# Fold products by column halves, an earlier fetch of source rows and one more batch of picks in a graph attention kernel

## The chip, the cores and the metric

The kernel runs on one core of a Trainium2 chip. The metric is the device time of one execution in microseconds (us); three runs give 1699.82, 1701.03 and 1702.28, median 1701.03. All numbers on single instructions come from one profiled execution.

## The reference

One layer of a graph network: 6250 nodes with 64 values each, 206250 edges sorted by destination, four heads of 16 values. The inputs `x`, `src`, `dst`, the edges' own values and the weights are given.

```
Qh, Kh, Vh = x @ W.T + b            # for each node, [N, 4, 16]
Ee = edge_attr @ We.T + be          # for each edge
score = (Kh[src] * Qh[dst] / 4 * Ee).sum(-1)
score = exp(clip(score, -5, 5))
wV = segment_sum(Vh[src] * score, dst)
out = layernorm(x + wV)
```

So for each edge the key and value row of its source is fetched, multiplied with the query of its destination, and the result is summed over the edges of one destination.

## The kernel before

**Tiles, groups, steps.** 128 edges are a tile, 8 tiles a group: 1612 tiles, 202 groups, the last of 4 tiles. Groups go in steps: two groups each at first, one each for the last eight (`STEPS`). A table of key and value rows of all nodes (`kv_tab`) is made first, then the main loop over `g` (line 983) runs an order written out by hand; each engine works off its own instructions in that order. Semaphores join them.

**Rows of the sources** come in two ways. POOL fetches a tile's 128 rows by an indirect DMA (`gather_kv`, L276), five steps of buffers ahead at most (`KVB`), one instruction per tile. Two tiles of most groups are not gathered but *picked*, that is, computed on TensorE: one batch makes four tiles, two each of two groups (`PICKED`). For a batch the source numbers are loaded to all partitions (`fetch_sources`, L236, a 256 KB DMA on SP's queue with two buffers), turned into `from`, `over` (ACT, L241, L242) and `odd` (DVE, L243) by `sources`; then DVE compares them with the node numbers (`hots`, L681) and PE multiplies these one-hot columns with the nodes' values `x`, held as three bf16 parts (`picks`, through `product`, L725, output `pick`). A batch has 25 units; a unit is three products of 128 rows by 512 columns (two for the last). 35 units go into 4 groups. After the last unit of a batch follow `picked` (DVE, L703), `picked_kv` (eight f32 products, `pick<-w,x`) and `place_kv` (ACT, L720), which writes the picked rows to the same buffers as the gathers do.

`LAST` (line 91) is the number of batches: as long as the group that ends a batch's units is more than 8 groups from the end. Here there are 67; the last units stand in group 192, and the last picked groups are 196 and 197. `BEGIN` and `READY` are the groups with a batch's first and last unit. 1304 gathers are left, besides the five first groups, whose rows are fetched otherwise.

**One iteration `g`** (lines 983 to 1092), as far as it matters here. SP: edges (`et`, every second group), sources if the next group begins a batch (line 994), queries (`qw`), keys (`kb`). PE: up to four units of picks, the turn of group `g+1` (L761: transposes `term` to `qe`), queries of `g+2` (`qq`), the other picks, a fold if one is due, the sums of a step (`sums`, `room<-msg,of`, 64-column halves in turn), edge products of `g+3` (`room<-et,we_sb`, four quadrants). DVE: `prod` and `score` of group `g` (`products`, L787, L789), what is left of the message of `g-1` (`take`, L827), the term of `g+1` (`terms`, L755), one-hot columns, the message of `g` (L808), and the adds. ACT: scores, copies (`keep`, L822), biases and one-hot rows. The gathers for the step four ahead are tied to marks on PE's products (`gather`).

**Folds.** Sums of a step land in a ring of 64-row blocks. After every some eight groups (24 times in all; `FOLDS`) `fold_blocks` brings two blocks of 128 rows together on PE, in f32: for each half `u` of the columns one product with `fold` (64 columns wide, L725 `room<-ring,fold`) and, into the first 31 rows of the same half, one or two with `ident` (`room<-ring,ident`). An f32 product is two instructions. Both halves stand in one PSUM bank, in partitions 0 to 63 and 64 to 127; `add_blocks` (L927) adds them to the output.

**The end.** From iteration 193 on there are no picks. Iterations 200 and 201 finish the last two groups; `last_add` (L963), the norms and two stores of the output (L959) follow.

Of the kernel before, what the change touches and what calls it, by code (L numbers as in the profile page):

```python
# [24 lines left out]
NG = -(-T // G)  # L25
# [32 lines left out]
def tiles_of(g):  # L58
    return min(G, T - g * G)
# [13 lines left out]
UNITS = NB // 2  # L73
# [7 lines left out]
def first_unit(g):  # L81

    return (g - LEAD) * 35 // 4


def when(k):

    return max(g for g in range(LEAD + 4 * k // 35 + 2) if first_unit(g) <= k)


LAST = max(m for m in range(1, NG) if when(UNITS * m - 1) + 8 < NG)
BEGIN = [when(UNITS * m) for m in range(LAST)]
READY = [when(UNITS * m + UNITS - 1) for m in range(LAST)]
PICKED = [(READY[m] + 4, READY[m] + 5) for m in range(LAST)]
ALL_PICKED = {g for pair in PICKED for g in pair}
assert len(ALL_PICKED) == 2 * LAST and min(ALL_PICKED) > XG
assert all(BEGIN[m + 1] > BEGIN[m] + 1 for m in range(LAST - 1))

# [36 lines left out]
def tile_gnn(ctx: ExitStack, tc: tile.TileContext, x, x_blocks, by_rows, xT, wT, bias, beT, weT, eT, src, src_rows, dst,  # L135
# [19 lines left out]
    def kv_of(g):  # L155

        s = max(s for s in range(NS) if STEPS[s][0] <= g)
        j = (g - STEPS[s][0]) * G
        return kvs[s % KVB][:, j:j + G, :]
# [52 lines left out]
    def fetch_edges(q):  # L212

        lo, hi = q * LG * G // 2, min((q + 1) * LG * G, T) // 2
        et = loads.tile([P, LG * G // 2, P], F32, name="et")
        nc.sync.dma_start(et[:, :hi - lo, :], eT[:, lo:hi, :])
        for g in range(q * LG, min((q + 1) * LG, NG)):
            ET[g] = et[:, (g % LG) * G // 2:(g % LG + 1) * G // 2, :]
# [13 lines left out]
    def fetch_sources(m, pool):  # L232

        if m < LAST:
            SRC[m] = pool.tile([P, BATCH * P], I32, name="srcs")
            nc.sync.dma_start(SRC[m], src_rows[m:m + 1, :].to_broadcast([P, BATCH * P]))  # L236
# [67 lines left out]
    with tc.tile_pool(name="nodes", bufs=1) as nodes, \  # L304
# [13 lines left out]
        slots = [kv.rearrange("p t c -> p (t c)") for kv in kvs]  # L318
# [163 lines left out]
        for i in range(NB // CB):  # L482
            bs = slice(i * CB, (i + 1) * CB)
            kv_sb = chunks.tile([P, CB, 2 * C], F32, name="kv_sb")
            for b in range(0, CB, 2):
                two = slice(i * CB + b, i * CB + b + 2)
                ps = npsum.tile([P, 2, 3 * C], F32, name="ps")
                for u in range(2):
                    c0 = (i * CB + b + u) * P
                    mark.append(nc.tensor.matmul(ps[:, u, :], xT_sb[:, c0:c0 + P], w_sb, start=True,  # L490
                                                 stop=True))
# [135 lines left out]
    with tc.If(rv == 0) as branch:  # L627

        with tc.tile_pool(name="work", bufs=2) as work, \
# [87 lines left out]
            def place_kv(m):  # L717
                for i, g in enumerate(PICKED[m]):
                    n = tiles_of(g)
                    nc.scalar.activation(kv_of(g)[:, n - 2:n, :], rooms_of(m)[:, 2 * i:2 * i + 2], AF.Copy)  # L720
# [3 lines left out]
            def product(*aps, **kw):  # L724
                mark.append(nc.tensor.matmul(*aps, **kw))  # L725
# [25 lines left out]
            def terms(g):  # L751

                n = tiles_of(g) // 2
                TERM[g] = work.tile([P, G // 2, P], F32, name="term")
                nc.vector.tensor_mul(TERM[g][:, :n], EB.pop(g)[:, :n], qq[:, :n])  # L755
# [24 lines left out]
            def some_of(g):  # L780

                n = tiles_of(g)
                return [(0, n)] if g < NG - 1 else [(0, n // 2), (n // 2, n)]

            def products(g, lo, hi):
                prod = work.tile([P, G, C], F32, name="prod", bufs=1)[:, :hi - lo, :]
                nc.vector.tensor_mul(prod, kv_of(g)[:, lo:hi, :C], qe[g % 2][:, lo:hi, :])  # L787
                SCORE[g] = work.tile([P, G, H], F32, name="score", bufs=3)[:, :hi - lo]
                nc.vector.tensor_reduce(SCORE[g], prod.rearrange("p g (h d) -> p g h d", h=H),  # L789
                                        axis=AX.X, op=OP.add)  # L790

            def weigh(g, lo, hi):
                score = SCORE.pop(g)
                nc.scalar.activation(score, score, AF.Relu, bias=five_p, scale=-1.0)  # L794
                WEIGHT[g] = weights[g % 3][:, lo:hi]
                nc.scalar.activation(WEIGHT[g], score, AF.Exp, bias=five_p, scale=-1.0)  # L796
# [23 lines left out]
            def keep(g, i):  # L820
                left, part = part_of(g, i)
                nc.scalar.activation(part, left, AF.Copy)  # L822
# [79 lines left out]
            def slots(lo, apart):  # L902

                ks = [k for k in (lo, lo + 2) if k in touched]
                if not apart and len(ks) == 2 and ks[0] % RING < ks[1] % RING:
                    return [(0, 2, ring[:, ks[0] % RING:ks[1] % RING + 1:2, :])]
                return [((k - lo) // 2, (k - lo) // 2 + 1, ring[:, k % RING:k % RING + 1, :]) for k in ks]

            def fold_blocks(i):

                for u in range(2):
                    whole = slots(4 * i + u, False)
                    for lo, hi, what in whole:
                        product(folded[u * C:(u + 1) * C, lo:hi], fold, what, start=True, stop=False,
                                skip_group_check=True)
                    for lo, hi, what in slots(4 * i + u - 1, i == len(ENDS) - 1):
                        product(folded[u * C:u * C + SHIFT, lo:hi], ident[:, C:C + SHIFT], what,
                                start=hi > max(h for _, h, _ in whole), stop=True, skip_group_check=True)

            def add_blocks(i):  # L920

# [61 lines left out]
            for g in range(NG + 1):  # L983
                now, before = g < NG, g > 0
# [6 lines left out]
                    going = alone(going[:2] if g == groups_of(step_of[g])[0] else going[2:])  # L991
                if g % LG == 0 and g + 3 * LG < NG:
                    fetch_edges(g // LG + 3)
                if g + 1 in BEGIN[1:]:
                    fetch_sources(BEGIN.index(g + 1) + 1, work)
                if g + 4 < NG:
                    fetch_queries(g + 4)
                if g % 2 == 0 and g + 6 < NG:
# [5 lines left out]
                where.append(mark[-1])  # L1004
                if former:
                    keep(g - 1, 1)
                if now:
                    products(g, *some_of(g)[0])
                if former:
                    take(g - 1, 1)  # L1010
                if g + 1 < NG:
                    terms(g + 1)
                if now:
                    weigh(g, *some_of(g)[0])
                if g + 2 < NG:
# [36 lines left out]
                if g in FOLDS:  # L1052
                    fold_blocks(FOLDS[g])
# [219 lines left out]
```

## Time and profile before

| | |
|---|---|
| median of three runs | 1701.03 us |
| the profiled execution | 1701.22 us |
| its span, first to last instruction | 1699.4 us |
| granted clock of TensorE, mean | 0.982 |
| gathers on POOL | 1304 of 946 ns |
| picks on PE | 4958 products |
| folds | 24 |

A busy share is that of the whole span. In a row of the page stand line, engine, operation, what it writes and reads, the count, the busy time with the mean of one, and the idle time just before with what ended most of it. In a row of the timeline stand the start, the length, engine, line and operation; a number in brackets is the engine's idle time just before, and what ended it. Rows of the stretches hold the stretch, its length, busy time of PE, weight loads, DVE, ACT and POOL, the granted clock, and the DMA engines' share and GB/s.

### The profile page before, as it was taken

What the parts mean: (1) busy time and instruction counts of PE and PEld (TensorE: products, weight loads), DVE (VectorE), ACT (ScalarE), POOL (GpSimd) and SP (SyncE); (2) the same over time, 40 slices, a digit from 0 to 9 for tenths busy, and PEclk for the clock granted to TensorE, in tenths of its full rate; (3) what the DMA queues carried; (4) which work ended last, traced back from release to release, by engine and by line L of the source; (5) the groups of instructions that cost most, each with busy time, mean ns of one, the idle gap of its engine ahead of it and who ended that gap; (6) DMA issues with size and microseconds to landing.
All of it is one profiled execution on the core that took longest, in us unless ns stands there. A gap on an engine that the chain in (4) does not pass through costs nothing.

```text
span 1699.4 us, 29987 instructions
## 1 busy us (share of the span) xinstructions
PE 1641.8 (97%) x10327; PEld 818.4 (48%) x10327; DVE 1525.8 (90%) x2588; ACT 1097.8 (65%) x1860; POOL 1272.5 (75%) x1354
## 2 busy tenths in 40 slices
PE   7799999999999999999999999999999999999975
PEld 6444444444444444444444444444444444444443
DVE  5699989899989899998998998989999999889986
ACT  3676666666666666666666666666666666666664
POOL 7777777777777777777777777777777777777775
PEclk9799999999999999999999999999999999999995
DMA  6744344343443434434434344443444433434341
GB/s 195 244 123 143 99 123 123 104 124 109 114 123 104 123 108 114 124 117 123 114 108 130 99 122 122 106 124 105 117 123 117 123 111 111 123 105 130 111 116 46
DMA packets 115090, 203.90 MB, mean 120 GB/s; under 512 B 55216, under 2 KB 55961, under 8 KB 114815
## 3 DMA queue, kind: packets, MB, share of 16 engines
q1 hardware_dynamic: 71484, 113.99, 22.1%
q0 software_dynamic: 43008, 86.86, 19.3%
q8 instruction: 83, 1.36, 0.3%
q10 hardware_dynamic: 436, 1.04, 0.3%
q14 instruction: 79, 0.65, 0.1%
HBM read 194.18 MB, written 7.59 MB: 119 GB/s over the span
## 4 chain that ended last, share of the span: by engine, by line
PE 80%; DVE 7%; DMA 7%; issue 2%; ACT 2%; POOL 1%; SPq 0%; DVEq 0%; ACTq 0%; POOLq 0%
PE pick L725 59%; PE room L725 11%; PE qe L761 5%; DMA kv<-kv_tab,src_i 4%; PE qq L725 3%; DMA srcs<-in_src_rows 2%; POOL kv L276 1%; DVE prod L787 1%; DVE msg L827 1%; DVE term L755 1%; PE ps L490 1%; DVE hot L681 1%; DVE score L789 1%; DVE qe L827 1%; DVE of L775 1%
## 5 line engine op out<-in xcount | busy, mean ns | idle before, releaser
L276 POOL DMA_INDIRECT kv<-kv_tab,src_i x1304 | 1233.1, 946 | 398.1 <-issue 173.8
L725 PE MATMUL pick<-hot,parts 128*128 128x512 bf16 x4958 | 1136.4, 380 | 0.0
L725 PEld LDWEIGHTS <-parts 128*128 128x128 bf16 x4958 | 459.5, 98 | 588.1 <-issue 90.3
L681 DVE TENSOR_TENSOR hot<-from,still 128x2560 bf16<-128x2560 bf16 (+4 forms) x415 | 481.7, 1164 | 2.4 <-ACT still L796 2.4
L822 ACT ACTIVATE msg<-qe 128x512 bf16<-128x512 f32 x400 | 237.8, 594 | 170.2 <-DVE qe L808 98.8
L740 ACT ACTIVATE eb<-room,be_col 128x512 f32<-128x512 f32 x202 | 136.8, 677 | 147.1 <-PE room L725 146.6
L262 ACT ACTIVATE to<-to,one_p 126x1024 bf16<-126x1024 bf16 x198 | 226.9, 1146 | 0.0
L256 ACT ACTIVATE to<-kb,minus_row 126x1024 bf16<-126x1024 uint8 x198 | 224.7, 1135 | 0.0
L794 ACT ACTIVATE score<-score,five_p 128x32 f32<-128x32 f32 x203 | 65.1, 321 | 147.8 <-DVE score L789 145.9
L761 PE MATMUL qe<-ident,term 128*128 128x128 f32 x806 | 125.7, 279 | 28.1 <-DVE term L755 26.4
L787 DVE TENSOR_TENSOR prod<-kv,qe 128x512 f32<-128x512 f32 x203 | 137.1, 676 | 12.0 <-PE qe L761 3.7
L789 DVE TENSOR_REDUCE score<-prod 128x32 f32<-128x512 f32 x203 | 138.5, 682 | 7.0
L827 DVE TENSOR_TENSOR qe<-qe,msg 128x512 f32<-128x512 f32 x200 | 138.2, 691 | 3.9 <-ACT msg L822 3.8
L808 DVE SCALAR_TENSOR_TENSOR qe<-still,kv 128x512 f32<-128x512 f32 x200 | 138.7, 693 | 0.8 <-ACT still L796 0.8
L827 DVE TENSOR_TENSOR msg<-qe,msg 128x512 bf16<-128x512 f32 x200 | 136.6, 683 | 3.1 <-ACT msg L822 2.6
L755 DVE TENSOR_TENSOR term<-eb,qq 128x512 f32<-128x512 f32 x202 | 136.6, 676 | 3.0 <-DMA kv<-kv_tab,src_i 2.6
L725 PE MATMUL room<-et,we_sb 64*64 64x256 f32 (+1 forms) x1616 | 136.2, 408 | 0.3 <-ACT eb L740 0.2
L761 PEld LDWEIGHTS qe<-ident,term 128*128 128x128 f32 x806 | 99.9, 143 | 75.8 <-DVE term L755 41.9
L243 DVE TENSOR_SCALAR odd<-srcs 128x512 int32<-128x512 int32 x66 | 30.2, 458 | 79.4 <-DMA srcs<-in_src_rows 79.3
L725 PE MATMUL room<-msg,of 128*64 128x192 bf16 (+1 forms) x1592 | 88.6, 251 | 1.6 <-DVE y L927 1.3
L725 PEld LDWEIGHTS <-of 128*64 128x64 bf16 (+1 forms) x1600 | 67.4, 110 | 39.0 <-issue 36.6
L241 ACT ACTIVATE from<-srcs,from_row 128x512 bf16<-128x512 int32 x66 | 47.3, 717 | 60.0 <-DMA srcs<-in_src_rows 60.0
(156 smaller groups left out, 1102.9 us busy)
## 6 DMA issues: line engine op xcount, KB each, us to landing
et<-in_eT SPq DMA_DIRECT2D x100, 512.0 KB
kb<-key_tab SPq DMA_DIRECT2D x101, 252.0 KB
kv<-kv_tab,src_i POOLq DMA_INDIRECT x1304
srcs<-in_src_rows SPq DMA_DIRECT2D x67, 256.0 KB
qw<-q_tab SPq DMA_DIRECT2D x202, 15.8 KB
kv_tab<-kv_sb SPq DMA_DIRECT2D x4, 640.0 KB
q_tab<-q SPq DMA_DIRECT2D x5, 480.0 KB
out<-y SPq DMA_DIRECT2D x2, 512.0 KB
```

The costliest lines, as they stand in the source:

```text
L256: nc.scalar.activation(TO[g][:, :n, :], KB.pop(g)[:, :n * P].rearrange("p (j e) -> p j e", j=n), AF.Square, bias=minus_row3[:3 * W])
L262: nc.scalar.activation(TO[g][:, :n, :], TO[g][:, :n, :], AF.Relu, bias=one_p[:3 * W], scale=-1.0)
L276: return nc.gpsimd.indirect_dma_start(out=kv_of(g)[:, j, :], out_offset=None, in_=kv_tab[:, :], in_offset=bass.IndirectOffsetOnAxis(ap=src ...
L681: nc.vector.tensor_tensor(HOT[k][:, lo_ - lo:hi_ - lo].rearrange("p b (a c) -> p b a c", c=2), pairs(from_)[:, None].to_broadcast(shape), ...
L725: mark.append(nc.tensor.matmul(*aps, **kw))
L755: nc.vector.tensor_mul(TERM[g][:, :n], EB.pop(g)[:, :n], qq[:, :n])
L761: nc.tensor.transpose(qe[g % 2][:, k:k + half + 1:half, :], TERM[g][:, k, :], ident)
L787: nc.vector.tensor_mul(prod, kv_of(g)[:, lo:hi, :C], qe[g % 2][:, lo:hi, :])
L789: nc.vector.tensor_reduce(SCORE[g], prod.rearrange("p g (h d) -> p g h d", h=H), axis=AX.X, op=OP.add)
L808: nc.vector.scalar_tensor_tensor(to.rearrange("p g (h d) -> p g h d", h=H), WEIGHT.pop(g)[:, :, :, None].to_broadcast([P, n, H, D]), LEAST ...
L822: nc.scalar.activation(part, left, AF.Copy)
L827: nc.vector.tensor_sub(left if i == 0 else part_of(g, 2)[1], left, part)
```

## The change

There are four edits.

1. `LAST` goes by 5 instead of 8 groups from the end. That makes 68 batches. The units of the new one stand in groups 192 to 195. `PICKED` lies four groups behind `READY` as before, but no further than group 199: the new batch fills two tiles each of groups 199 and 200. The other batches stay as they are.
2. `fold_blocks` makes the `fold` products of both halves first and then the `ident` products of both; before, one half came after the other.
3. `fetch_sources` is called two groups ahead of `BEGIN`, not one.
4. In iteration 200 alone (`NG - 2`) `products` comes behind `take` and `terms`.

```diff
-LAST = max(m for m in range(1, NG) if when(UNITS * m - 1) + 8 < NG)
+LAST = max(m for m in range(1, NG) if when(UNITS * m - 1) + 5 < NG)
-PICKED = [(READY[m] + 4, READY[m] + 5) for m in range(LAST)]
+PICKED = [(r + k, r + k + 1) for r in READY for k in [min(4, NG - 2 - r - 1)]]
...
             def fold_blocks(i):
 
+                whole = [slots(4 * i + u, False) for u in range(2)]
                 for u in range(2):
-                    whole = slots(4 * i + u, False)
-                    for lo, hi, what in whole:
+                    for lo, hi, what in whole[u]:
                         product(folded[u * C:(u + 1) * C, lo:hi], fold, what, start=True, stop=False,
                                 skip_group_check=True)
+                for u in range(2):
                     for lo, hi, what in slots(4 * i + u - 1, i == len(ENDS) - 1):
                         product(folded[u * C:u * C + SHIFT, lo:hi], ident[:, C:C + SHIFT], what,
-                                start=hi > max(h for _, h, _ in whole), stop=True, skip_group_check=True)
+                                start=hi > max(h for _, h, _ in whole[u]), stop=True,
+                                skip_group_check=True)
...
-                if g + 1 in BEGIN[1:]:
-                    fetch_sources(BEGIN.index(g + 1) + 1, work)
+                if g + 2 in BEGIN[1:]:
+                    fetch_sources(BEGIN.index(g + 2) + 1, work)
...
-                if now:
+                if now and g != NG - 2:
                     products(g, *some_of(g)[0])
                 if former:
                     take(g - 1, 1)
                 if g + 1 < NG:
                     terms(g + 1)
+                if g == NG - 2:
+                    products(g, *some_of(g)[0])
                 if now:
                     weigh(g, *some_of(g)[0])
```

## Prediction

> **What bounds the kernel now.** I read the page first, then who waited for whom, the busy time by stretches, and the timeline around one fold and at the end.
>
> ```profile
> span 1699.4 us, 29987 instructions
> PE 1641.8 (97%) x10327; PEld 818.4 (48%) x10327; DVE 1525.8 (90%) x2588; ACT 1097.8 (65%) x1860; POOL 1272.5 (75%) x1354
> L276 POOL DMA_INDIRECT kv<-kv_tab,src_i x1304 | 1233.1, 946 | 398.1 <-issue 173.8
> ```
> ```profile
> POOL kv L276 <- issue: 173.8, 568, 0.5
> ```
>
> POOL looks 75% busy, but the gather row says otherwise: 1304 gathers, 946 ns each, and 398.1 us idle before them, which is 0.305 us for each one. The longest such gap was 0.5 us. So POOL issues a gather every 1.25 us from its first to its last and never really waits: it is full, and its last gather can only come earlier if there are fewer.
>
> ```profile
> 115.00:1636.00 1521.00, 1514.05 (x9679) 733.26 (x9678) 1396.56 (x2274) 995.29 (x1646) 1150.14 (x1217) 1.00 0.41 117
> 1636.00:1683.00 47.00, 26.13 (x205) 15.68 (x203) 40.11 (x85) 31.84 (x54) 35.42 (x39) 0.79 0.32 89
> PE qe L761 <- DVE term L755: 5.7, 11, 1.0
> ```
>
> From 115 to 1636 us PE is busy 1514 of 1521 us (the first column behind the stretch's length), and waits for DVE 5.7 us in all (the waits of that same stretch). So the long middle goes at PE's pace. Then the picks end, PE falls to 26 of 47 us, and DVE (40 of 47) sets the pace. How far POOL leads can be read from the last gather of a group and the group's `prod` (L787, one per group in order; gathers counted back from the last, 4, 8 or 6 to a group): here group 189 and group 200.
>
> ```profile
> 1585.23 0.94 POOL L276 DMA_INDIRECT kv<-kv_tab,src_i  x1 [0.30 <-PE pick L725]
> 1605.55 0.69 DVE L787 TENSOR_TENSOR prod<-kv,qe 128x512 f32<-128x512 f32 x1
> ...
> 1680.09 0.94 POOL L276 DMA_INDIRECT kv<-kv_tab,src_i  x1 [0.30 <-issue]
> 1683.09 0.69 DVE L787 TENSOR_TENSOR prod<-kv,qe 128x512 f32<-128x512 f32 x1 [3.13 <-issue]
> ```
>
> The lead is 20.3 us at group 189 and gone at group 200: there DVE idles 3.13 us and starts 3.0 us after the last gather began. I read that 3.0 as the landing. So **two clocks meet at group 200**: POOL's gathers, and the chain of PE and DVE, which would have been ready at 1683.09 - 3.13 = 1679.95. From there 16.3 us follow to the end at 1699.4.
>
> **The change, part by part.**
>
> *Fewer gathers.* With the sixth last group as bound there are 68 batches, not 67. The new one picks two tiles each of groups 199 and 200, so POOL does 1300 gathers. Four times 1.25 is 5.0 us. Two go before group 199's last gather and two before group 200's, so group 200's data can be there at 1683.09 - 5.0 = 1678.1, and group 201's also 5.0 earlier. Nothing on POOL hides or adds to this.
>
> *More picks.* The new batch has 25 units, 24 of three products and one of two: 74 products, in iterations 192 to 195, where none or few stand now.
>
> ```profile
> 1628.81 0.60 PE L761 MATMUL qe<-ident,term 128*128 128x128 f32 x4
> 1629.68 3.41 PE L725 MATMUL pick<-hot,parts 128*128 128x512 bf16 x15
> 1633.02 0.66 PE L725 MATMUL room<-et,we_sb 64*64 64x256 f32 x8
> ...
> 1639.30 0.66 PE L761 MATMUL qe<-ident,term 128*128 128x128 f32 x4 [1.10 <-DVE term L755]
> 1642.43 1.16 PE L725 MATMUL pick<-w,x 128*128 128x128 f32 x8 [1.40 <-ACT pick L714]
> 1645.25 0.66 PE L761 MATMUL qe<-ident,term 128*128 128x128 f32 x4 [1.66 <-DVE term L755]
> 1650.25 0.66 PE L761 MATMUL qe<-ident,term 128*128 128x128 f32 x4 [1.38 <-DVE term L755]
> 1655.90 0.68 DVE L755 TENSOR_TENSOR term<-eb,qq 128x512 f32<-128x512 f32 x1
> ```
>
> A run of 15 picks takes 1633.02 - 1629.68 = 3.34 us, 0.223 each; 74 are 16.5 us. All stand between the turns (L761) of group 192 (1628.81) and group 196 (1650.25). In that stretch PE waits 1.10 + 1.40 + 1.66 + 1.38 = 5.5 us, which the picks fill; so group 196's turn comes 16.5 - 5.5 = 11 us later. DVE, which now trails PE there, has caught up by then: behind that turn (0.66) it has prod, score, take and term, some 2.5 us, and ends group 197's term at 1650.25 + 11 + 0.66 + 2.5 = 1664.4, against 1655.90 + 0.68 = 1656.6 now: 7.8 later. The new batch's `x` (L703, 0.74 for one in the tail) comes after that. I take 8.5 us; the bounds are 11.7 (nothing caught up) and 2 (the hots, 7.7 us a batch by the row below, less the waits of 5.5 us). That POOL itself slows under more DVE work can be left out: its gathers take 0.94 us beside the hots and in the tail alike.
>
> ```profile
> L681 DVE TENSOR_TENSOR hot<-from,still 128x2560 bf16<-128x2560 bf16 (+4 forms) x415 | 481.7, 1164 | 2.4 <-ACT still L796 2.4
> 842.93 0.43 PE L725 MATMUL room<-ring,fold 128*64 128x128 f32 x2
> 843.29 0.41 PE L725 MATMUL room<-ring,ident 128*31 128x64 f32 x4
> 843.63 0.43 PE L725 MATMUL room<-ring,fold 128*64 128x128 f32 x2
> 844.00 0.41 PE L725 MATMUL room<-ring,ident 128*31 128x128 f32 x2
> 844.33 0.85 PE L725 MATMUL room<-msg,of 128*64 128x192 bf16 x16
> 845.11 0.66 PE L725 MATMUL room<-et,we_sb 64*64 64x256 f32 x8
> L725 PE MATMUL room<-ring,fold 128*64 128x128 f32 (+1 forms) x96 | 20.8, 299 | 0.0
> ```
>
> *Folds.* A fold is four phases one after another, 0.36 + 0.34 + 0.36 + 0.34 = 1.40 us: the sum for the lower column half, its shifted rest, the same for the upper half. The change puts the two sums next to each other, then the two rests. The `sums` right behind show what neighbours in different column halves do: 16 products of 192 columns in 0.78 us, where a full-width pick of 512 columns at 0.223 would make 0.084 for each and 1.34 for 16. So they run side by side, as the four quadrants of L725 `et` do. With each pair side by side, two phases are left: 0.70 us saved a fold. 96 instructions are 24 folds (two halves, two passes); 22 lie before 1636. The saving S by then is 22 x 0.70 = 15.4 us; its bounds are 0 and 15.4. I take 15.4, by the nearest row.
>
> Against it stands the Trainium skill, "TensorE: Matmul & The Clock Gate", Part 3: weights load beside a running product only when the row groups differ. The two sums share all their rows; by that rule nothing is saved and the kernel ends where the third rival puts it. The `sums` share their rows too, and the trace does not bear the rule out there.
>
> *Sources a group earlier.* This moves the 67 loads of `srcs` (one DMA issue each) one iteration ahead on SP, past the loads of queries and keys of one iteration (and, every second time, of edges).
>
> ```profile
> DVE odd L243 <- DMA srcs<-in_src_rows: 79.3, 35, 3.7
> ```
>
> DVE stands still 79.3 us for it, 35 times. But PE has felt little: at most the 5.7 us above. So the gain is between 0 and 5.7 us of PE's time; I take 0, since POOL will be the bound. What slips behind a load on SP slips by one issue, and is used an iteration or more later.
>
> *Group 200's products behind group 201's term.* Now DVE waits for the gathers with take and term still to do.
>
> ```profile
> 1680.35 0.58 ACT L822 ACTIVATE msg<-qe 128x512 bf16<-128x512 f32 x1
> ...
> 1685.34 0.69 DVE L808 SCALAR_TENSOR_TENSOR kv<-still,kv 128x512 f32<-128x512 f32 x1
> 1685.48 0.69 PE L761 MATMUL qe<-ident,term 128*128 128x128 f32 x2 [5.40 <-DVE term L755]
> 1685.96 1.49 PE L725 MATMUL pick<-msg,of 128*128 128x192 bf16 x8
> 1687.24 3.57 PE L725 MATMUL pick<-kv,kv 128*128 128x64 f32 x16
> 1692.55 0.28 DVE L963 SCALAR_TENSOR_TENSOR y<-qq,above,y 128x64 f32<-128x64 f32 x1 [0.72 <-PE qq L725]
> ```
>
> In front of prod now come the wait for ACT's copy (to 1680.93), take (0.6) and term (0.4): DVE is ready for prod at 1682.0 instead of 1679.95, 2.05 later. In return the turn of 201 and the sums of 199 (1685.48 to 1687.24) are done before the data come. Those of 200 then start behind their message (1685.34 + 0.69 = 1686.03) and not at 1687.24, PE ends 1.2 us earlier, and the last add, which waits 0.72 us for it, loses that wait: -0.7 us (bounds 0 and -0.72, as the other work of DVE stands right before).
>
> **The sum.** Data of group 200: 1678.1. PE and DVE: 1679.95 + 8.5 + 2.05 - S = 1690.5 - S, with S = 15.4: 1675.1. The data are later, by 3 us; prod starts at 1678.1, 5.0 earlier, and the end loses 0.7 more: 5.7 us. PE's gain eats the lead (20.3 - 15.4 = 4.9 at group 189, still over 3.0); were it eaten up earlier, DVE would wait for gathers, but POOL would end no later. The profiled execution took 1701.22 us, 0.2 over the median 1701.03, which I use: **1695.3 us**. Every S above 12.4 gives the same.
>
> **Rivals.**
>
> *The halves stay in turn and only the switches go.* A second product of a kind then needs its two passes alone. A pass of 128 columns in f32 is 1.00 / 8 = 0.125 us, by this run of eight:
>
> ```profile
> 835.13 1.16 PE L725 MATMUL pick<-w,x 128*128 128x128 f32 x8
> 836.13 2.75 PE L725 MATMUL pick<-hot,parts 128*128 128x512 bf16 x12
> ```
>
> The pairs then take 0.36 + 0.25 and 0.34 + 0.25, and a fold saves 0.20: S = 4.4, prod at 1686.1, 3.0 later, less 0.7: 1703.3 us. For it: these are f32 products of two passes, the sums bf16 of one. Against it: the quadrants of `et` are f32, and their eight passes of 256 columns took 0.66 us, where one after another at 0.25 they would take 2.0. With one of the two pairs side by side a fold saves 0.45: S = 9.9, prod at 1680.6, 2.5 earlier and the 0.7: 1697.8 us.
>
> *The tail's DVE becomes the bound.* At the upper bound of the added work (11.7) prod is ready at 1678.3 with full S, just with the data: no loss. With S at 12 as well it comes at 1681.7: 1.4 earlier and the 0.7, 1699 us.
>
> *The folds save nothing*, the change not doing what it says. Then S = 0, prod at 1690.5 against 1683.09: 7.4 later, less 0.7, 1707.7 us: slower. The end is later than before with S under 6.7, that is 0.30 us a fold, and by more than 0.2% with S under 3.3.
>
> **How the numbers follow.** Forecast 0.73, the tail's DVE 0.07, halves in turn 0.06, one pair 0.05, nothing saved 0.09. 0.2% is 3.4 us, about what a measurement of this kernel can tell from no change: faster is below 1697.6, slower above 1704.4. Faster: 0.75 (the forecast and a little of the second); slower 0.09; the rest, 0.16, is the same. The forecast's own range is 1694 to 1697; 8 in 10 takes in the DVE case and part of the halves: 1694.0 to 1701.0.
>
> **What would show it.** Two starts of the fold phases within some nanoseconds, and 0.7 us from the first fold to the `sums`. POOL's last gather at about 1680, with no gap over 0.5 us. A lead of some 5 us at group 189, and L787 of groups 198 to 200 waiting for the gathers. No wait of L243 for `srcs`. L963 without its wait for PE. It is wrong if POOL pauses (then its last gather says so), or if the last prods wait for PE's turns, not for data.

## The result and the profile after

The changed kernel takes 1695.35 us (median of six runs, 1694.53 to 1696.01), the kernel before 1701.23 beside it (six runs, 1699.82 to 1702.69): ratio 0.9965, 95% interval 0.9952 to 0.9978. The profiled execution took 1695.44 us. The forecast was 1695.3, so the sum came out. Whether its terms did is another question, and one of them did not.

First the page of the changed kernel: its span, its engines, its gathers. (From `fold_blocks` on its line numbers are two higher: the last add is L965, `add_blocks` L929.)

```profile
span 1693.4 us, 30174 instructions
PE 1638.0 (97%) x10409; PEld 817.2 (48%) x10409; DVE 1536.2 (91%) x2597; ACT 1086.7 (64%) x1865; POOL 1269.1 (75%) x1350
L276 POOL DMA_INDIRECT kv<-kv_tab,src_i x1300 | 1229.7, 946 | 396.7 <-issue 176.7
```

Then POOL's waits, the long stretch, and the one line of the sources in the groups by line.

```profile
POOL kv L276 <- issue: 176.7, 578, 0.5
```
```profile
115.00:1636.00 1521.00, 1516.32 (x9798) 736.39 (x9796) 1415.52 (x2300) 993.42 (x1666) 1150.10 (x1217) 1.00 0.41 118
```
```profile
L243 DVE TENSOR_SCALAR odd<-srcs 128x512 int32<-128x512 int32 x67 | 29.7, 443 | 0.0
```

The shares look as before. What moved is small: 1300 gathers at the old pitch, (1229.7 + 396.7) / 1300 = 1.251 us, none with a gap over 0.5; in the same middle stretch PE gets through 9798 instructions, where it was 9679; and `odd` (L243) no longer waits for `srcs`.

One fold on PE's timeline, and the `fold` products among the groups by line:

```profile
830.51 0.44 PE L725 MATMUL room<-ring,fold 128*64 128x128 f32 x4
830.88 0.42 PE L725 MATMUL room<-ring,ident 128*31 128x64 f32 x6
831.23 0.85 PE L725 MATMUL room<-msg,of 128*64 128x192 bf16 x16
```
```profile
L725 PE MATMUL room<-ring,fold 128*64 128x128 f32 (+1 forms) x96 | 10.5, 299 | 0.0
```

From the first sum to the `sums` behind the fold it is now 831.23 - 830.51 = 0.72 us, where it was 1.40. The 96 `fold` instructions take as long each as before (299 ns), but their busy time together is 10.5 us where it was 20.8: they lie on top of each other in pairs.

Where the two clocks meet, on the timelines of POOL and DVE (the last gather of group 189 and its `prod`; `prod` of group 198; the last gather of group 200, what DVE does then, and POOL's very last gather):

```profile
1585.59 0.94 POOL L276 DMA_INDIRECT kv<-kv_tab,src_i  x1 [0.30 <-PE qe L761]
1588.25 0.69 DVE L787 TENSOR_TENSOR prod<-kv,qe 128x512 f32<-128x512 f32 x1 [1.04 <-DMA kv<-kv_tab,src_i]
...
1663.70 0.69 DVE L787 TENSOR_TENSOR prod<-kv,qe 128x512 f32<-128x512 f32 x1 [2.74 <-issue]
...
1675.47 0.94 POOL L276 DMA_INDIRECT kv<-kv_tab,src_i  x1 [0.30 <-issue]
1677.92 0.41 DVE L755 TENSOR_TENSOR term<-eb,qq 128x256 f32<-128x256 f32 x1
1678.47 0.69 DVE L787 TENSOR_TENSOR prod<-kv,qe 128x512 f32<-128x512 f32 x1
1680.47 0.94 POOL L276 DMA_INDIRECT kv<-kv_tab,src_i  x1 [0.30 <-PE pick L725]
```

The last gather of group 200 starts 1680.09 - 1675.47 = 4.6 us earlier and `prod` of that group 1683.09 - 1678.47 = 4.6: they go together, 3.0 apart both times. At group 189 DVE waits for a gather already, with a lead of 2.7 us. The term of group 201 ends at 1678.33, 0.14 us before `prod`: in group 200 the two clocks arrive almost together, because DVE had been held for the gathers in group 198 (2.74 us) and needs two iterations of some 7.4 us from there. POOL needs as long: with two tiles picked, groups 199 and 200 have six gathers each, 7.5 us at 1.25. So by these numbers, from group 198 on, neither clock gains on the other, and more picked tiles in these two groups alone would bring little; that was not run.

The end, on the timelines of PE and DVE:

```profile
1678.39 0.69 PE L761 MATMUL qe<-ident,term 128*128 128x128 f32 x2 [1.95 <-DVE term L755]
1678.87 1.49 PE L725 MATMUL pick<-msg,of 128*128 128x192 bf16 x8
1681.34 3.68 PE L725 MATMUL pick<-kv,kv 128*128 128x64 f32 x16 [0.98 <-DVE kv L808]
1687.00 0.25 DVE L965 SCALAR_TENSOR_TENSOR y<-qq,above,y 128x64 f32<-128x64 f32 x1
```

The turn and the sums of 199 are done before the message of 200 comes (PE waits 0.98 us for it), and the last add has no wait for PE. From `prod` of 200 to the last add it is 8.53 us, before 9.46: 0.9 less.

### The profile page after: what moved, and what is told of

Its sections match the earlier page's. It is cut to its first block, busy times and chain, and to the rows that moved or that the text cites. A ratio compares the mean times of both kernels' runs of the same rounds, so it can differ in the third digit from the quotient of the medians.

```text
span 1693.4 us, 30174 instructions
## 1 busy us (share of the span) xinstructions
PE 1638.0 (97%) x10409; PEld 817.2 (48%) x10409; DVE 1536.2 (91%) x2597; ACT 1086.7 (64%) x1865; POOL 1269.1 (75%) x1350
## 3 DMA queue, kind: packets, MB, share of 16 engines
q8 instruction: 83, 1.36, 0.3%
## 4 chain that ended last, share of the span: by engine, by line
PE 88%; DVE 5%; DMA 3%; issue 1%; ACT 1%; POOL 0%; DVEq 0%; SPq 0%; ACTq 0%; POOLq 0%
PE pick L725 66%; PE room L725 12%; PE qe L761 5%; PE qq L725 4%; DMA kv<-kv_tab,src_i 2%; PE ps L490 1%; DVE prod L787 1%; DVE term L755 1%; DVE msg L827 1%; DVE hot L681 1%; DVE score L789 1%; DMA ones_tab<-ones 0%; POOL kv L276 0%; DMA et<-in_eT 0%; DMA w_sb<-in_bias 0%
## 5 line engine op out<-in xcount | busy, mean ns | idle before, releaser
L276 POOL DMA_INDIRECT kv<-kv_tab,src_i x1300 | 1229.7, 946 | 396.7 <-issue 176.7
L725 PE MATMUL pick<-hot,parts 128*128 128x512 bf16 x5032 | 1153.0, 380 | 0.0
L725 PEld LDWEIGHTS <-parts 128*128 128x128 bf16 x5032 | 466.2, 98 | 596.5 <-issue 91.4
L681 DVE TENSOR_TENSOR hot<-from,still 128x2560 bf16<-128x2560 bf16 (+4 forms) x421 | 487.9, 1162 | 2.4 <-ACT still L796 2.4
L761 PE MATMUL qe<-ident,term 128*128 128x128 f32 x806 | 124.7, 278 | 24.2 <-DVE term L755 22.7
L761 PEld LDWEIGHTS qe<-ident,term 128*128 128x128 f32 x806 | 100.6, 143 | 69.3 <-DVE term L755 32.9
L725 PE MATMUL qq<-to,qw 126*64 126x512 bf16 x396 | 80.9, 405 | 0.0
L725 PE MATMUL pick<-w,x 128*128 128x128 f32 x544 | 78.8, 288 | 1.1 <-ACT pick L714 1.1
```

The costliest lines, as they stand in the source:

```text
L276: return nc.gpsimd.indirect_dma_start(out=kv_of(g)[:, j, :], out_offset=None, in_=kv_tab[:, :], in_offset=bass.IndirectOffsetOnAxis(ap=src ...
L681: nc.vector.tensor_tensor(HOT[k][:, lo_ - lo:hi_ - lo].rearrange("p b (a c) -> p b a c", c=2), pairs(from_)[:, None].to_broadcast(shape), ...
L761: nc.tensor.transpose(qe[g % 2][:, k:k + half + 1:half, :], TERM[g][:, k, :], ident)
```

## The experiments

The theory to test (P): the end follows the later of two clocks, POOL's gathers and the chain of PE and DVE; folds and sources only make room on the second for the batch that takes gathers from the first. Rivals: the gathers alone set the end (G); PE's work sets it all along, each microsecond saved there showing at the end (E); others are told in the expectations. "Turn 192" is PE's L761 for group 192, "data" the start of the last gather of group 200; all times in us, each ratio with the kernel before beside it on the same chip. The runs come from several chips (the four with parts of the change left out from one, on which the kernel before took 1703.14 us; it took 1702.88 and 1703.53 beside the later ones), so medians of different rows are best compared by their ratios.

| kernel | gathers | turn 192 | data | `prod` of 200 | last add | median | ratio to before, 95% |
|---|---|---|---|---|---|---|---|
| before | 1304 | 1628.81 | 1680.09 | 1683.09 | 1692.55 | 1701.23 | |
| after | 1300 | 1609.23 | 1675.47 | 1678.47 | 1687.00 | 1695.35 | 0.9965 (0.9952 to 0.9978) |
| batch and order alone | 1300 | 1630.75 | 1676.20 | 1692.90 | 1701.43 | 1710.43 | 1.0046 (1.0029 to 1.0062) |
| folds and sources alone | 1304 | 1608.52 | 1680.03 | 1682.92 | 1692.38 | 1701.51 | 0.9986 (0.9978 to 0.9995) |
| after, old folds | 1300 | 1617.45 | 1676.66 | 1679.60 | 1688.13 | 1696.16 | 0.9956 (0.9941 to 0.9971) |
| after, old fetch | 1300 | 1621.25 | 1675.75 | 1682.71 | 1691.23 | 1698.96 | 0.9975 (0.9964 to 0.9985) |
| after, old order in 200 | 1300 | 1609.61 | 1675.44 | 1678.20 | 1687.69 | 1696.58 | 0.9964 (0.9952 to 0.9976) |
| after, 8 gathers fewer | 1292 | 1601.87 | 1666.76 | 1669.57 | 1678.90 | 1687.34 | 0.9903 (0.9888 to 0.9918) |
| after, one more batch | 1296 | 1612.41 | 1670.64 | 1676.70 | 1685.23 | 1694.52 | 0.9943 (0.9929 to 0.9956) |
| the same, queries behind the picks | 1296 | 1605.05 | 1670.46 | 1674.04 | 1682.57 | 1691.35 | 0.9934 (0.9921 to 0.9948) |

### The batch and the order alone

The kernel before with edits 1 and 4, without the folds and the earlier fetch:

```diff
-LAST = max(m for m in range(1, NG) if when(UNITS * m - 1) + 8 < NG)
+LAST = max(m for m in range(1, NG) if when(UNITS * m - 1) + 5 < NG)
...
-                if now:
+                if now and g != NG - 2:
                     products(g, *some_of(g)[0])
```

> The kernel before with the added batch and the moved products alone; folds and sources stay as before. Theory P (two clocks meet at group 200: POOL's gathers, and the chain of PE and DVE, 1690.5 - S): S is 0, so group 200's prod starts at about 1690.5, 7.4 us later than before, and the end loses 0.7 to 1.4: 1707 to 1708 us, slower by 0.4%. L787 of group 200 does not wait for gathers. Rival G (the number of gathers alone sets the end): 1695 to 1696 us. Rival E (PE sets the end everywhere, each edit counts with its time on PE): 16.5 us more, 1717 us.

Its turn 192, and its timeline at group 200:

```profile
1630.75 0.60 PE L761 MATMUL qe<-ident,term 128*128 128x128 f32 x4
...
1676.20 0.94 POOL L276 DMA_INDIRECT kv<-kv_tab,src_i  x1 [0.30 <-issue]
1692.57 0.41 DVE L755 TENSOR_TENSOR term<-eb,qq 128x256 f32<-128x256 f32 x1
1692.90 0.68 DVE L787 TENSOR_TENSOR prod<-kv,qe 128x512 f32<-128x512 f32 x1
```

The data lie ready for 13 us; `prod` has no idle time before it and comes behind the term. 1710.43 us, slower than before: G falls. From turn 192 to `prod` it is 62.15 us; before it was 1628.81 to 1679.95, the point where DVE would have been ready, 51.1. The batch and the order therefore cost 11.0 us of the tail (10.55 was taken); another 1.9 had been lost ahead of group 192, where these two edits change nothing. That loss stands in iterations in which DVE waits for `srcs` (2.3 us between groups 10 and 192; DVE waits 86.6 us for them in all, before 79.3). The kernel before itself took 1703.14 us beside this run, 1.9 more than beside the changed kernel, so the loss need not come from the edits.

### The folds and the sources alone

The kernel before with edits 2 and 3:

```diff
+                whole = [slots(4 * i + u, False) for u in range(2)]
...
-                if g + 1 in BEGIN[1:]:
+                if g + 2 in BEGIN[1:]:
```

> The kernel before with the folds by halves in turn and the earlier sources alone; 67 batches and 1304 gathers as before. Theory P: PE's middle gets 20 to 25 us faster, but POOL's last gather stays where it was: 1701 us, no change; the lead at group 189 falls from 20 us to 3 or 4. Rival E: 1676 to 1681 us, faster by over 1%.

```profile
1680.03 0.94 POOL L276 DMA_INDIRECT kv<-kv_tab,src_i  x1 [0.30 <-issue]
1682.92 0.69 DVE L787 TENSOR_TENSOR prod<-kv,qe 128x512 f32<-128x512 f32 x1 [4.55 <-issue]
```

PE is 20.3 us ahead of before at turn 192 (1608.52 against 1628.81), and 0.2 us of it are left at group 200, where DVE idles 4.55 us for the gathers. The ratio is 0.9986: 0.14% less time (0.05 to 0.22%), where E asks for over 1%. E falls. Together these two runs show that neither half of the change brings by itself what the whole does.

### After, with the old folds

```diff
-                    for lo, hi, what in whole[u]:
+                    whole = slots(4 * i + u, False)
+                    for lo, hi, what in whole:
...
-                for u in range(2):
```

> The changed kernel with the folds as before. The sources alone gave PE 7 to 9 us between groups 10 and 150 in the changed kernel's trace, so 10 to 11 by group 192. Theory P: prod of group 200 at 1690.5 - 10.5 = 1680, against 1678.5 in the changed kernel: 1.5 us slower, 1696 to 1698 us. Rival E: 24 folds of 0.69 us are lost, 1711 to 1712 us. Rival G: 1695.4 us.

```profile
1617.45 0.60 PE L761 MATMUL qe<-ident,term 128*128 128x128 f32 x4
...
1676.66 0.94 POOL L276 DMA_INDIRECT kv<-kv_tab,src_i  x1 [0.30 <-issue]
1679.60 0.68 DVE L787 TENSOR_TENSOR prod<-kv,qe 128x512 f32<-128x512 f32 x1
```

Turn 192 at 1617.45 and the 62.15 us of the tail give 1679.60, and the data with 3.0 give 1679.7: a tie. 1696.16 us; the interval contains the 0.9965 of the whole change. So with the sources early the folds are hardly needed: the time doesn't show them. Against batch and order alone, run beside it on the same chip, the sources have brought PE 1630.75 - 1617.45 = 13.3 us by group 192; of the 13.5 that the two differ by between groups 10 and 192, 12.3 stand in iterations in which DVE stood for `srcs` without them. This I had costed at nothing.

### After, with the old fetch

```diff
-                if g + 2 in BEGIN[1:]:
-                    fetch_sources(BEGIN.index(g + 2) + 1, work)
+                if g + 1 in BEGIN[1:]:
+                    fetch_sources(BEGIN.index(g + 1) + 1, work)
```

> The changed kernel with the sources fetched as before. Theory P: the folds alone give S = 22 x 0.69 = 15.2, prod could start at 1675.3, the gathers land at 1678.4: the same as the changed kernel, 1695.4 us, with a lead of about 5 us at group 189. Rival E: 10 us slower, 1705 us.

This one missed in the trace. Its timeline at group 200, its sources by line, and PE's waits between 115 and 1500 us:

```profile
1675.75 0.94 POOL L276 DMA_INDIRECT kv<-kv_tab,src_i  x1 [0.30 <-issue]
1682.71 0.68 DVE L787 TENSOR_TENSOR prod<-kv,qe 128x512 f32<-128x512 f32 x1
```
```profile
L243 DVE TENSOR_SCALAR odd<-srcs 128x512 int32<-128x512 int32 x67 | 30.5, 455 | 82.5 <-DMA srcs<-in_src_rows 82.5
```
```profile
PE qe L761 <- DVE term L755: 8.5, 13, 1.7
```

`prod` comes 4.2 us later than in the whole change and 7.0 after the last gather: the chain is last again. The profiled execution took 1700.05 us; the twelve spread from 1696.27 to 1702.56, and the ratio, 0.9975 (0.9964 to 0.9985), overlaps that of the whole change. So the miss rests on this one trace more than on the times. Against batch and order alone the folds bring 1630.75 - 1621.25 = 9.5 us by group 192, not 15.4, though each fold is as short as in the changed kernel. The waits tell where the rest went: PE's wait for terms is 8.5 us where it was 6.6 without the faster folds:

```profile
PE qe L761 <- DVE term L755: 6.6, 11, 1.2
```

(The row is from the same stretch of batch and order alone.) Counted from turn to turn over groups 10 to 150, the faster folds save 11.65 us in the 17 iterations with a fold, and 3.8 of it are lost again, 3.0 in iterations in which DVE stands for `srcs`: PE comes earlier to a wait that stays. With the early sources the same folds save 11.6 and nothing is lost.

What one such wait does is seen in group 71 of batch and order alone, and in the same iteration with the sources early (the changed kernel with the old folds):

```profile
635.91 0.60 PE L761 MATMUL qe<-ident,term 128*128 128x128 f32 x4
639.64 0.43 DVE L243 TENSOR_SCALAR odd<-srcs 128x512 int32<-128x512 int32 x1 [4.30 <-DMA srcs<-in_src_rows]
643.82 0.55 PE L761 MATMUL qe<-ident,term 128*128 128x128 f32 x3 [1.21 <-DVE term L755]
```
```profile
632.44 0.60 PE L761 MATMUL qe<-ident,term 128*128 128x128 f32 x4
638.99 0.60 PE L761 MATMUL qe<-ident,term 128*128 128x128 f32 x4
```

DVE stands 4.30 us for `srcs`, its term ends late, and PE's next turn comes after 7.91 us, not 6.55. The loss of 1.36 is 0.15 more than the 1.21 that the row shows as idle. The likely reason lies in the rows: the ends of products are modelled, and a run of 12 picks is listed as 2.75 us long where the turn behind it starts after 2.59 us without any wait (1602.32 and 1604.91 in the kernel before). These 0.16 us are lost too when PE has to wait, but the row counts them as busy.

### Runs on another chip

The next four ran on a chip where the kernel before took 2046.45 us: instructions lasted about as long as elsewhere (a pick 391 ns for 380), but stood further apart. Of the old order in iteration 200, by line:

```profile
L276 POOL DMA_INDIRECT kv<-kv_tab,src_i x1300 | 1233.9, 949 | 721.6 <-issue 298.7 <-PE pick L725 158.7 <-PE room L725 94.0
```

A gather has 949 ns, but 0.555 us of idle time ahead of it in the mean, not 0.305, and PE is busy 88% of the span. In that trace PE stands idle 174 us in front of picks, `room` and turns for nothing that the profile shows, against 14 with the same kernel on a chip like the first. The times below were forecast for a chip like the first, and the theory's numbers don't hold there. So these runs decide nothing for it, and the same four kernels were run once more on chips like the first. What held PE was not found out.

The order of before in iteration 200:

> The changed kernel with group 200's products ahead of take and term, as before. Prod of group 200 starts at 1678.4 either way. Theory P: the sums of groups 199 and 200 come later on PE again and the last add waits for them: 0.7 to 1.4 us slower than the changed kernel, 1696.1 to 1696.8 us. Rival: the order there is worth nothing, 1695.4 us.

2045.52 us, ratio 1.0002 (0.9991 to 1.0013).

Eight gathers left out:

> The changed kernel with 8 of the 1300 gathers left out (the last two tiles of four groups near group 100, whose edges then use rows that an earlier group left in the buffer). Theory P: POOL ends 10.0 us earlier; PE and DVE would be ready for group 200 at 1690.5 - 24 = 1666, the gathers at 1668.5: 1685 to 1686 us. Rival H (PE and DVE stand right behind POOL now, the lead being used up): 1692 to 1695 us.

2033.6, ratio 0.9931 (0.9907 to 0.9956).

One more batch by a higher density of units:

> The changed kernel with 53 units to 6 groups for 35 to 4: 69 batches, 1296 gathers, the last units in group 196. POOL ends 5.0 us earlier, PE has 16.5 us of picks and 1.0 us of picked products more. Theory P: PE and DVE had 12 us in hand and now are ready at 1666 + 17.5 = 1683.5, 5 us after the changed kernel's 1678.5: 1700 to 1701 us. Rival G (gathers alone): 1690.4 us.

2041.82, ratio 0.9985 (0.9969 to 1.0001).

The same with the queries behind all picks:

> The same with the products of the queries (64 columns wide) behind all picks, next to the folds and sums, which are 64 columns wide too. Each pass between products of the full width and narrower ones costs PE about 0.1 to 0.15 us in the trace, and one pair goes in most iterations: 19 to 28 us for PE. Theory P: PE and DVE ready at 1683.5 - 19 = 1664.5 or earlier, the gathers at 1673.5: POOL sets the end again, 1690 to 1691 us. Rival: no gain on PE from the order, 1700 to 1701 us as with one more batch alone.

2038.76, ratio 0.9965 (0.9953 to 0.9977).

### The order of before in iteration 200

```diff
-                if now and g != NG - 2:
+                if now:
                     products(g, *some_of(g)[0])
...
-                if g == NG - 2:
-                    products(g, *some_of(g)[0])
```

> The changed kernel with group 200's products ahead of take and term, as before, once more on a chip on which the gathers follow each other at 1.25 us. Theory P: 0.7 to 1.4 us slower than the changed kernel, ratio to the kernel before 0.9970 to 0.9974 where the changed kernel had 0.9965. Rival: the order there is worth nothing, 0.9965.

```profile
1678.20 0.69 DVE L787 TENSOR_TENSOR prod<-kv,qe 128x512 f32<-128x512 f32 x1 [1.91 <-DMA kv<-kv_tab,src_i]
1680.58 0.69 PE L761 MATMUL qe<-ident,term 128*128 128x128 f32 x2 [4.17 <-DVE term L755]
1681.06 1.49 PE L725 MATMUL pick<-msg,of 128*128 128x192 bf16 x8
1682.34 3.57 PE L725 MATMUL pick<-kv,kv 128*128 128x64 f32 x16
```

Here DVE idles 1.91 us for the gathers, with take and term still to do, and PE's turn and the sums of 199 stand ahead of those of 200 (1682.34 against 1681.34 with the order changed). From `prod` to the last add it is 9.49 us instead of 8.53. The trace shows the 0.96; the times (0.9964 against 0.9965) can't tell it.

### Eight gathers fewer

The changed kernel without the last two gathers of four groups near 100. Their edges use the rows of an earlier group, so the output is not that of the layer; only the times are of use:

```diff
-            js = [j for j in range(tiles_of(g)) if not is_picked(g, j)]
+            js = [j for j in range(tiles_of(g)) if not is_picked(g, j) and not (g in LEFT and j >= G - 2)]
```

> The changed kernel with 8 of the 1300 gathers left out (the last two tiles of four groups near group 100, whose edges then use rows that an earlier group left in the buffer), once more. Theory P: POOL ends 10.0 us earlier, PE and DVE are ready for group 200 at 1692.9 - 26 = 1667, the gathers at 1668.5: 1685 to 1686 us, ratio 0.9906. Rival H (PE and DVE stand right behind POOL): 1692 to 1695 us.

Its last gather of group 200 and the `prod`:

```profile
1666.76 0.94 POOL L279 DMA_INDIRECT kv<-kv_tab,src_i  x1 [0.30 <-issue]
1669.57 0.69 DVE L790 TENSOR_TENSOR prod<-kv,qe 128x512 f32<-128x512 f32 x1 [0.33 <-DMA kv<-kv_tab,src_i]
```

The gather starts 8.7 us earlier than in the changed kernel (10.0 forecast, at 1.25; from first to last the gathers of this execution follow each other at 1.2523 us for 1.2511, which makes 1.5), `prod` 8.9, the last add 8.1. So in the changed kernel the gathers are still what holds the end, and the chain of PE and DVE has about 9 us in hand; the near tie in group 200 was DVE held by the gathers two groups before.

### One more batch

Picks instead of gathers, by a density of 53 units in 6 groups instead of 35 in 4; 69 batches:

```diff
-    return (g - LEAD) * 35 // 4
+    return (g - LEAD) * 53 // 6
```

> 69 batches and 1296 gathers, queries where they were, once more. POOL could end 5.0 us earlier. PE and DVE: with the added batch and products alone prod of group 200 stood at 1692.9, folds and sources together are worth 26 us, one more batch costs 17.5: 1684.4, against 1678.5 in the changed kernel. Theory P: 6 us slower than the changed kernel, 1701 us, ratio to the kernel before about 1.000, and prod of group 200 does not wait for gathers. Rival G (gathers alone): 1690 to 1691 us, 0.9936.

```profile
1670.64 0.94 POOL L276 DMA_INDIRECT kv<-kv_tab,src_i  x1 [0.30 <-issue]
1676.37 0.41 DVE L755 TENSOR_TENSOR term<-eb,qq 128x256 f32<-128x256 f32 x1
1676.70 0.68 DVE L787 TENSOR_TENSOR prod<-kv,qe 128x512 f32<-128x512 f32 x1
```

The kind is right: `prod` comes behind the term with data ready since about 1673.6. The size missed by 7.7 us (`prod` 1676.70, not 1684.4): PE had more in hand than I reckoned. 1694.52 us; the last add comes 1.8 us earlier than in the changed kernel, and by the times the two can't be told apart (0.9929 to 0.9956 against 0.9952 to 0.9978).

### One more batch, queries behind the picks

If the chain is last there, time off PE should come out. The queries of `g+2` (two products of 64 columns) now stand behind the picks, next to the `sums` or the fold, not between the turn and the picks:

```diff
-                if g + 2 < NG:
-                    queries(g + 2)
                 for some in two[2:]:
                     picks(some)
                     where.append(mark[-1])
+                if g + 2 < NG:
+                    queries(g + 2)
```

> 69 batches, 1296 gathers, and the products of the queries behind all picks, once more. In the first trace of this order the turn took 437 ns to the next start for 530, and the queries 240 for 339 where the sums follow: some 0.15 us for PE per iteration, 27 us in all, against 17.5 us for the batch. Theory P: POOL still sets the end, 5.0 us earlier than in the changed kernel: 1690 to 1691 us, ratio 0.9936. Rival (DVE, which has 8.9 us more to do, becomes the bound in the tail): 1694 us or more.

```profile
1300.79 0.60 PE L761 MATMUL qe<-ident,term 128*128 128x128 f32 x4
1301.23 3.40 PE L725 MATMUL pick<-hot,parts 128*128 128x512 bf16 x15
1304.56 0.41 PE L725 MATMUL qq<-to,qw 126*64 126x512 bf16 x2
1304.80 0.83 PE L725 MATMUL room<-msg,of 128*64 128x192 bf16 x16
...
1670.46 0.94 POOL L276 DMA_INDIRECT kv<-kv_tab,src_i  x1 [0.30 <-issue]
1674.04 0.68 DVE L787 TENSOR_TENSOR prod<-kv,qe 128x512 f32<-128x512 f32 x1
```

The data come at the same time, `prod` 2.7 us earlier, 3.6 behind the last gather: the two clocks are nearly level again. 1691.35 us (1690.68 to 1691.9), ratio 0.9934: the shortest time of all kernels that compute the layer in full. Its interval lies below that of the changed kernel; against one more batch alone (0.9929 to 0.9956) the intervals overlap, and only the trace tells the two apart.

## Why the prediction was right, and where it was not

*The bound.* Right. POOL never pauses, and the data of group 200 came with the last gather at 1675.47 (1675.1 forecast), `prod` at 1678.47 (1678.1). Leaving out eight more gathers moved the last add by 8.1 us; giving PE 20 us without taking gathers away moved it by 0.2 us, and the time by 0.14%.

*The added batch.* Right: 11.0 us of the tail with the reordered products, 10.55 taken; without the room for it the kernel took 1710.43, where the rival in which the folds save nothing had 1707.7 (by the ratio, 1.0046 of 1701.03, it is 1708.9). The hots' 7.7 us a batch take in two smaller rows of L681; the row shown, 481.7 us for 67 batches, gives 7.2. Only the lower bound of 2 hangs on it.

*The folds.* Right in size, 0.68 us each for 0.70. Two f32 products in different column halves run side by side, though they share their rows. The Trainium skill, "TensorE: Matmul & The Clock Gate", Part 3, has weights load beside a running product only where the row groups differ; by that line the pairs would have saved nothing, and the measurement decides against it here. The same part's table has three column tiles run 2.38 times as fast, which goes the way of the measurement: it is this one line that the folds contradict.

*The sources.* Wrong, and this is the step that failed: "the gain is between 0 and 5.7 us of PE's time; I take 0". It was 13.3 by group 192 against the run beside it, 11.4 (1628.81 - 1617.45) against the kernel before itself. The bound was PE's visible wait for one name, the terms. Three things are missing from it. PE also waits at other places when DVE is late, as the kernel before shows in the same view:

```profile
PE pick L725 <- ACT pick L714: 1.0, 3, 0.5
```

Each wait costs some 0.15 us more than its row shows. These two make most of it: in batch and order alone the waits between 115 and 1636 us are 7.3 us for terms and 1.6 for `pick`, 15 in all, and with 0.15 for each that is 11.2 of the 13.3. And a wait grows when PE comes earlier: with the faster folds the terms' was 8.5 between 115 and 1500 us, not 6.6.

*S.* Wrong therefore in its parts. The folds alone gave 9.5 us by group 192 (15.4 less the ones that the stalls took back), under the 12.4 that the sum said it needs; and without the sources the kernel took 1698.96. So the forecast of the whole came out partly by luck: an edit costed at nothing brought 13.3 us. Had the change been folds, batch and order without the sources, the same sum would have said 1695.3 and been off by 3.7 us, or by 1.5 if the ratio is taken (0.9975 of 1701.03 is 1696.8).

*The lead.* It was eaten sooner than forecast: 2.7 us at group 189, not some 5, with DVE waiting for gathers there already. PE gained 19.6 us by turn 192, held there by the gathers: with eight fewer it had gained 26.9 (1601.87), about what 22 folds at 0.68 (15.0) and the 11.4 of the sources add up to. *The last prods* were to wait for gathers in groups 198 to 200; 198 did by 2.74 us, 200 by 0.14 at most. The 3 us of slack that the sum put between the chain and the data in group 200 were not there in the trace, though for a reason within the theory: the chain had been held two groups earlier.

*The end.* Forecast 0.7 less, 0.9 found to the last add, by the runs with and without the order 0.96.

*Open* is why `srcs` came later in batch and order alone than in the kernel before, and what held PE on the other chip.

## What to carry to other kernels

Read a queue's gaps, not its busy share: an engine that is 75% busy with a constant 0.3 us between instructions is full. Where two engines each have a clock of their own, find the point at which they meet; time saved on the one that isn't last buys nothing but room to move work over from the other, so the saving and the moved work have to come together. And a wait seen on an engine does not bound what the removal of its cause brings: here the rows showed 8.9 us where 13.3 were to be had, and savings on the same engine make such a wait longer, so that several at once are not a sum.

## What the runs showed of the hardware

What stands next to what costs PE some 0.1 us. In the changed kernel the queries, products of 64 columns, stand between the full-width turn and the full-width picks:

```profile
1282.35 0.60 PE L761 MATMUL qe<-ident,term 128*128 128x128 f32 x4
1282.88 0.41 PE L725 MATMUL qq<-to,qw 126*64 126x512 bf16 x2
1283.22 3.41 PE L725 MATMUL pick<-hot,parts 128*128 128x512 bf16 x15
```

From the turn to the queries it is 0.53 us and from the queries to the picks 0.34. In the last experiment, in the rows shown there, it is 1301.23 - 1300.79 = 0.44 from the turn to the picks and 1304.80 - 1304.56 = 0.24 from the queries to the `sums`; both are the commonest values between 115 and 1500 us. Where the edge products follow the queries there, in quadrants of 64 rows by 64 columns, it is 0.34 again. So a passage between full-width and 64-column products seems to cost 0.09 to 0.10 us. The Trainium skill, "TensorEngine Tiling (Array Packing)", Key Properties, says that a change of tiling mode drains the array; these numbers agree with it, though no run here changed the width alone.

The chip of the second set took 20% longer for the same kernel, with instructions of nearly the same length (a gather 949 ns for 946, a pick 391 for 380) and longer gaps between them. A time without its neighbour from the same chip says little.
